# Two attention blocks with Fourier convolutions on one core: transposes in row halves, X in quarters, one batch's x by DRAM, and a new order of the steps

## The chip, the cores and the metric

The kernel runs on one core of a Trainium2 chip. The metric is the device time of one execution in microseconds; the time before is the median of three runs. The profile shows one execution, taken by the hardware profiler, with a span of 457.4 us. TensorE is called PE there, VectorE DVE, ScalarE ACT, GpSimd POOL and SyncE SP; PEld is TensorE's weight load.

## The reference

x has the shape (2, 56, 128, 128), float32: 2 batches of 56 planes of 128 x 128. Two layers of the same form, each with weights of its own, run after one another. In short:

```python
def fno_layer(x, w, b, sw, sb, norm=False, act=False):
    y = spectral_conv(x, w, b)      # rfft2, 2 x 16 x 16 modes mixed, irfft2
    if norm:
        y = inorm(y)
    y = y + skip1x1(x, sw, sb)
    return gelu(y) if act else y

xn = inorm(xa, g1, b1)              # xa: each plane an item of its own
k, q, v = (fno_layer(xn, ...) for K, Q, V)             # 8 heads each
attn = softmax(qh @ kh.T / sqrt(H * W))                # 56 x 56 per head
out = fno_layer(heads of attn @ vh, P...)
att = inorm(out + xa, gan, ban)
h = fno_layer(inorm(att, g2, b2), M0..., norm=True, act=True)
h = fno_layer(h, M1..., norm=True)
y = inorm(h, gmo, bmo) + att
```

What matters for the kernel: the Fourier convolutions touch only 512 modes a plane, the attention is a 56 x 56 matrix per head and batch, and all means and variances can be had from modes and from Gram matrices. So few passes over the planes remain: one that turns x to the front and takes statistics, one that makes the gelu, one that turns its result back and transforms it, and one that makes the layer's output.

## The kernel before

**Layout.** The planes of both batches lie in one buffer, X2: partition 64c + k holds plane k (56 of them) and one of two values c of a row index, so each row of X2 holds two image rows, one in each half of the partitions. The partitions 56 to 63 of each half are padding; row 56 carries a vector of scales. P[b] is a work buffer for each batch, xr holds three slices of 1024 columns for the x that is added at a layer's end, WU and WT hold built weights and later the intermediate results of the transforms. PSUM is handed out as single banks (two) and as pairs of banks (three).

**Steps.** Each piece of work is a Python generator, one for each layer and batch, with a letter. A `yield` ends one step. The string ORDER lists all steps of all generators, by letter and by 2 x layer + batch, so `t2` is a step of "turn" in layer 2, batch 0. At the end `_in_order` ties every engine to the order in which its instructions were written, so ORDER sets the queue of each engine.

- W, R, O, A, B, C: weights. GpSimd prepares the raw weights (prepare), TensorE spreads them over partitions (relay, L376), GpSimd builds the mode matrices (build, L387, and build_m).
- t, k, m, n, g, c: turn (transposes of X2, L412 in layer 1 and L414 in layer 2, ScalarE copies to P[b]), count (statistics, L425), the modes (L518, L435), normalise, the Gram matrix (L569) and its chain.
- q, u, s, v, a, d, p: scale_x (GpSimd scales X2 in place, L609), attention scores and values, softmax, heads and the norms. At the end of `values`, eight transposes of the modes (L694) give XT; at the end of softmax_chain eight products of XT with the matrix BT (L741) give pb.
- y, z, b, f, h: gelu (synthesis L816, mixed L831, gelu L847), its statistics (L854), turn_back (transposes L863, ScalarE copies L864), forward (L881) and the chain to the second norm (transposes of VectorE at L895, sums L487, inverse L452 and L457).
- x, e, o: the end of a layer. end_x fetches x (layer 1, by DMA from the input, L963; layer 2, by a GpSimd multiplication that undoes the scaling of X2, L969); end_sums makes synthesis and products, in layer 2 with a product that adds xr (L989); end_out finishes on VectorE (L1000), and in layer 1 GpSimd adds xr and writes X2 (L1002), while layer 2 sends the result out (L1005).

The transposes of layer 1's turn take 56 rows of either half of the partitions by themselves, each at a tile position of its own. The other transposes of planes (L414, L863) take 120 rows, both halves with the padding between, at once. The initial transfers are queued on SyncE: six of the eight parts of batch 0's x, then all constants but the identity in one transfer (L231, 888.5 KB), then the rest of batch 0, the small parameters and the raw weights of layer 1, and batch 1.

Of the kernel before, what the change touches and what calls it, by code (L numbers as in the profile page):

```python
# [37 lines left out]
F32 = mybir.dt.float32  # L38
# [11 lines left out]
for _name, _n in (  # L50
    ("ident", N), ("fw", 32), ("fh", N), ("gw", N), ("group", N), ("dup", N), ("ext", N), ("fold", 64),
    ("raw", 56), ("count", 8), ("syn", 1), ("same", 32), ("m8", 8), ("sel", 135), ("pick", 32), ("n2", 1), ("fx", N), ("gh", 2 * N),
):
    _PARTS[_name] = (sum(n for _, n in _PARTS.values()), _n)
# [89 lines left out]
t0 t0 t0 t0 t0 W0 t0 k0 k0 k0 k0 k0 t0 t0 k0 k0 k0 m0 m0 m0 W0 m0 m0 n0 n0 n0 t1 t1 t1 t1 m0 k1 k1 k1 t1 t1 m0 m0 W0  # L144
W0 t1 t1 W0 R0 R0 n0 n0 n0 R0 R0 R0 B0 k1 k1 g0 g0 k1 k1 g0 g0 g0 k1 g0 m1 B0 m1 g0 g0 A0 c0 m1 m1 C0 n1 n1 u0 u0 m1
n1 m1 n1 A0 A0 m1 n1 n1 q1 u0 u0 u0 g1 g1 m1 g1 g1 g1 c0 g1 g1 s0 A0 s0 s0 g1 B0 B0 x0 c1 u1 u0 q0 u0 u0 u1 u1 u1 u1
c0 C0 W1 W1 s1 s0 s0 s0 a0 s1 s1 W1 u1 u1 u1 O0 v0 a0 v0 v0 v0 v0 a0 W1 s1 W1 c1 x0 s1 c1 s1 a1 d0 d0 d0 d0 a0 a0 q0
v1 a1 p0 p0 v1 v1 p0 p0 q0 q0 v1 p0 v1 a1 d1 d1 d1 p0 p0 q0 a1 q0 d1 a1 p0 p0 R1 p1 q0 q0 R1 p1 p1 p1 y0 y0 y0 p1 b0
R1 R1 b0 z0 p1 p1 R1 R1 R1 y0 y0 y0 f0 f0 f0 q1 q1 q1 q1 p1 b0 b0 y0 y0 C1 z0 y0 f0 f0 q1 q1 q1 b0 b0 f0 z0 y0 y0 y0
f0 b0 z0 f0 b0 z0 p1 z0 z0 z0 f0 y1 y1 y1 f0 f0 y1 y1 y1 y1 y1 y1 b1 f0 h0 z1 z1 h0 h0 b1 h0 h0 h0 z1 z1 f1 f1 z1 f1  # L150
y1 h0 y1 y1 z1 z1 z1 b1 b1 h0 h0 f1 f1 b1 b1 f1 h0 f1 f1 f1 b1 h0 h0 b1 f1 h0 f1 f1 h1 h1 e0 e0 o0 e0 e0 o0 h1 h1 x0
x0 x0 e0 o0 x0 e0 o0 x0 t2 k2 A1 h1 h1 e0 h1 e0 o0 e0 o0 h1 h1 x0 e0 e0 o0 x1 t2 h1 e0 o0 h1 h1 h1 k2 t2 k2 A1 A1 A1
t2 t2 k2 x1 k2 e1 e1 e1 x1 t2 t2 o1 o1 t2 x1 e1 e1 e1 k2 k2 o1 o1 e1 k2 e1 e1 x1 o1 x1 m2 x1 x1 e1 o1 e1 o1 e1 m2 t3
o1 k3 m2 m2 m2 m2 n2 n2 n2 t3 t3 m2 t3 m2 k3 n2 k3 k3 B1 B1 t3 t3 t3 t3 k3 g2 g2 g2 g2 g2 k3 k3 g2 g2 u2 u2 k3 m3 m3
u2 u2 u2 m3 n3 m3 n3 m3 m3 n3 g2 c2 n2 n2 n3 m3 n3 m3 g3 g3 g3 g3 g3 c2 g3 B1 g3 g3 s2 s2 s2 s3 c3 u2 u2 u2 c2 s2 B1
O1 q2 q2 s2 c3 s2 q2 q2 u3 u3 q2 u3 u3 q2 u3 s3 s3 a2 u3 C1 v2 v2 v2 a2 u3 u3 v2 c3 s3 s3 v2 s3 a3 v3 v3 d2 d2 a2 d2
d2 a2 a2 p2 v3 a3 p2 p2 a3 p2 a3 v3 p2 v3 d3 d3 p2 p2 p2 n3 d3 d3 a3 p3 q2 q2 y2 y2 y2 p3 p3 p3 y2 y2 y2 b2 p2 x2 b2
z2 q3 q3 q3 q3 p3 y2 y2 q3 y2 f2 f2 b2 f2 b2 p3 p3 f2 f2 q3 f2 b2 b2 y2 q3 y2 z2 y2 z2 p3 f2 f2 b2 z2 z2 p3 b2 f2 q3
y3 y3 z3 x2 y3 z3 f2 f2 b3 y3 b3 y3 y3 f3 f3 b3 b3 z2 z2 f3 f2 h2 h2 x3 y3 h2 h2 y3 y3 z2 h2 f3 f3 f3 b3 y3 y3 z3 z3
z3 y3 f3 b3 b3 z3 f3 b3 f3 f3 f3 f3 h3 h3 h3 h2 h2 h2 h3 z3 z3 h3 h3 h3 h2 h3 h3 h2 h3 h2 h2 x2 x2 h3 h2 e2 e2 e2 e2  # L160
e2 x2 x2 x2 e2 o2 o2 o2 o2 h3 h3 e2 x2 e2 e2 x2 e2 e2 x3 e2 e3 e3 x3 x3 o2 x3 e3 x3 e3 e3 x3 o2 o2 o2 o3 o3 o3 e3 e3
e3 x3 e3 e3 o3 e3 x3 o3 o3 o3 e3 o3
# [19 lines left out]
def fno_layers(ctx: ExitStack, tc: tile.TileContext, x, out, weights, small, const):  # L182
# [10 lines left out]
    pq = pool("pair", 3, space=bass.MemoryType.PSUM)  # L193

# [22 lines left out]
    ident = C["ident"]  # L217
    S.dma_start(out=ident, in_=const["all"][:, :N])
# [4 lines left out]
    for b in range(B):  # L223
        for g in range(0, 8, 2):
            for c in range(2):
                Q.dma_start(
                    out=X2[64 * c : 64 * c + K, b, 8 * g : 8 * g + 16, :].rearrange("p (g r) w -> p g (r w)", r=8),
                    in_=xin[c, b, :, g : g + 2, :],
                )
            if (b, g) == (0, 4):  # L230
                Q.dma_start(out=Ct[:, N:], in_=const["all"][:, N:])  # L231
        if b == 0:
            for n in range(2):
                Q.dma_start(out=smt[n], in_=small[n : n + 1, :].to_broadcast([N, N_SMALL]))
            Q.dma_start(out=stage[:, :1088], in_=weights[0].rearrange("p m r n t -> p (m r n t)"))
# [17 lines left out]
    xr = cp.tile([N, 3, 1024], F32, name="xr")  # L253
    G.memset(xr.rearrange("p a b -> p (a b)"), 0.0)
# [145 lines left out]


    def turn(L, b):
        for g in range(8):
            p = pair()
            for s in range(2):
                for e in range(4):
                    i = 8 * g + 4 * s + e
                    if L == 0:
                        for c in range(2):
                            q = slice(64 * c, 64 * c + K)  # L410
                            o = K * (4 * s + e)
                            T.transpose(p[:, c, o : o + K], X2[q, b, i, :], ident[q, q], tile_position=(64 * c, 0))  # L412
                    else:
                        T.transpose(p[:, s, N * e : N * e + 120], X2[:120, b, i, :], ident[:120, :120])  # L414
            dst = P[b][:, 896 * g : 896 * g + 896].rearrange("p (x c k) -> p x c k", x=8, c=2)
            if L == 0:
                S.copy(dst.rearrange("p x c k -> p c x k"), p[:, :, :448].rearrange("p c (x k) -> p c x k", x=8))  # L417
            else:
                S.copy(dst, p.rearrange("p s (e c k) -> p (s e) c k", e=4, c=2)[:, :, :, :K])
            yield  # L420
# [196 lines left out]
    def room(b):  # L617
        R = P[b]
        return {
            "VT": R[:, :4096].rearrange("p (t m) -> p t m", t=4), "XT": R[:, 4096:5120].rearrange("p (t m) -> p t m", t=8),  # L620
            "AT": R[:, 5120:5344], "xs": R[:, 5344:5800], "SC": grid(R[:, 6912:7168], 4), "SG": grid(R[:, 7352:7800]),
            "MI": grid(R[:, 7800:8024], 4), "UX": [R[:, 896 * j : 896 * j + 896] for j in range(2)],
        }
# [52 lines left out]
    def values(L, b):  # L676
# [15 lines left out]
        p = pair()  # L692
        for t in range(8):
            T.transpose(p[:K, t // 4, N * (t % 4) : N * (t % 4) + N], xv[:, t, :], ident)  # L694
        S.copy(R["XT"][:K].rearrange("p t m -> p (t m)"), p[:K].rearrange("p j m -> p (j m)"))
        yield

    def softmax_chain(L, b):
# [40 lines left out]
        pb = s["pair"][:, 1]  # L739
        for t in range(8):  # L740
            T.matmul(pb[:, K * t : K * t + K], lhsT=XT[:K, t, :], rhs=BT[:, :K], start=True, stop=True)  # L741
        yield

    def heads(L, b):
        R = room(b)
        AT, VT = grid(R["AT"], 4), R["VT"].rearrange("p t (e u a m) -> p t e u a m", e=2, u=2, a=4)
        st[L][b]["pair"] = pair()
        p = st[L][b]["pair"][:, 0]
# [13 lines left out]
    def norms_chain(L, b):  # L762
        s, (par, d, _), R = st[L][b], prs[L], P[b]
        D, pb = s["D"], s["pair"][:, 1]
        Pm, u, y0, sqy, s1 = (R[:, 448 * j : 448 * j + 448] for j in range(5))
        bm = R[0:1, 5800:5856]
        V.tensor_tensor(Pm, pb[:, :448], D, ALU.add)
# [3 lines left out]
        V.tensor_tensor(pb[:, :448], pb[:, :448], Pm, ALU.add)  # L771
        V.tensor_tensor(u, pb[:, :448], D, ALU.mult)
# [84 lines left out]
    def turn_back(L, b):  # L857
        for n in range(8):
            p = pair()
            for r in range(2):  # L860
                for e in range(4):
                    o = 512 * r + N * e
                    T.transpose(p[:, r, N * e : N * e + 120], h3(b, n)[:120, o : o + N], ident[:120, :120])  # L863
            S.copy(  # L864
                hT[n % 2].rearrange("p r e c k -> p (r e) c k"),
                p.rearrange("p r (e c k) -> p (r e) c k", e=4, c=2)[:, :, :, :K],
            )
            yield
# [81 lines left out]
    far = [t.rearrange(f, A=4, j=4, c=2) for t, f in zip((x, out), forms)]  # L950

    def end_x(L, b):

        if L == 1:
            p = bank()
            T.matmul(p[:, :N], lhsT=st[L][b]["gv"].to_broadcast([N, N]), rhs=ident, start=True, stop=True)
            inv = st[L][b]["gvr"]
            V.reciprocal(inv, p[:, :N])
            yield
        for n in range(8):  # L960
            if L == 0:
                for c in range(2):
                    Q.dma_start(  # L963
                        out=xr[64 * c : 64 * c + K, n % 3, :].rearrange("p (r m) -> p r m", r=2),
                        in_=far[0][b, c, :, n // 2, 2 * (n % 2) : 2 * (n % 2) + 2],
                    )
            else:
# [4 lines left out]
                )  # L972
            yield

    def end_sums(L, b):
        s = st[L][b]
        for A in range(4):
# [4 lines left out]
            for v in range(2):  # L982
                n = 2 * A + v
                mixed(L, b, A, v, both[v], Be_[b], L == 0)
                if L == 1:
# [10 lines left out]
    def end_out(L, b):  # L996
        s = st[L][b]
        for n in range(8):
            h, p = h3(b, n), s["ends"][n]
            V.scalar_tensor_tensor(h, h, s["hs"], p.rearrange("p r m -> p (r m)"), ALU.mult, ALU.add)  # L1000
            if L == 0:
                G.tensor_tensor(X2[:, b, 8 * n : 8 * n + 8, :].rearrange("p e w -> p (e w)"), h, xr[:, n % 3, :], ALU.add)  # L1002
            else:
                for c in range(2):
                    Q.dma_start(  # L1005
                        out=far[1][b, c, :, n // 2, 2 * (n % 2) : 2 * (n % 2) + 2],
                        in_=h[64 * c : 64 * c + K].rearrange("p (r m) -> p r m", r=2),
# [75 lines left out]
```

## Time and profile before

Time before: 463.39 us, the median of 463.01, 463.39 and 463.41.

| Row of the profile | Count | Busy us | Mean ns |
|---|---|---|---|
| L863, TensorE transposes 120 x 128 of turn_back | 256 | 31.1 | 271 |
| L414, TensorE transposes 120 x 128 of layer 2's turn | 128 | 16.1 | 275 |
| L412, TensorE transposes 56 x 128 of layer 1's turn | 256 | 14.9 | 271 |
| L694, TensorE transposes 128 x 56 for XT | 32 | 4.2 | 276 |
| L741, TensorE products with BT | 64 | 8.0 | 275 |
| L989, TensorE products that add xr | 128 | 16.6 | 589 |
| L969, GpSimd multiplications for xr | 16 | 37.3 | 2360 |
| L1002, GpSimd additions of xr | 16 | 37.4 | 2369 |
| L1000, VectorE, end of a layer | 32 | 40.4 | 1275 |

How to read it: a matrix product in float32 shows as two records, a transpose as one. The busy time of a TensorE row is the union of records that overlap, so it is not the time that the row holds up the engine. Mean is the length of one record. The planes' transposes have nearly the same mean in both forms; how far apart they start is seen in the timeline alone. A line number belongs to the kernel before.

### The profile page before, as it was taken

What the parts mean: (1) busy time and instruction counts of PE and PEld (TensorE: products, weight loads), DVE (VectorE), ACT (ScalarE), POOL (GpSimd) and SP (SyncE); (2) the same over time, 40 slices, a digit from 0 to 9 for tenths busy, and PEclk for the clock granted to TensorE, in tenths of its full rate; (3) what the DMA queues carried; (4) which work ended last, traced back from release to release, by engine and by line L of the source; (5) the groups of instructions that cost most, each with busy time, mean ns of one, the idle gap of its engine ahead of it and who ended that gap; (6) DMA issues with size and microseconds to landing.
All of it is one profiled execution on the core that took longest, in us unless ns stands there. A gap on an engine that the chain in (4) does not pass through costs nothing.

```text
span 457.4 us, 14855 instructions
## 1 busy us (share of the span) xinstructions
PE 404.3 (88%) x6724; PEld 285.7 (62%) x6724; DVE 264.5 (58%) x457; ACT 186.8 (41%) x250; POOL 251.6 (55%) x263
## 2 busy tenths in 40 slices
PE   2347889999999999999899989999999999869994
PEld 1324668779886665756654858878857665554441
DVE  1438933114444479799889942223626788776653
ACT  2336333483404565612322634684265565320000
POOL 2089677999933930029889405954099200006693
PEclk9999899998978999999999999999979999859998
DMA  8999600000010020005444000000000000003565
GB/s 185 233 224 197 128 3 4 3 4 3 3 7 0 2 49 1 2 1 163 120 122 123 4 3 5 3 3 3 7 3 7 1 1 2 2 0 99 172 204 173
DMA packets 9887, 25.97 MB, mean 57 GB/s; under 512 B 1616, under 2 KB 2256, under 8 KB 9808
## 3 DMA queue, kind: packets, MB, share of 16 engines
q1 hardware_dynamic: 9680, 24.96, 22.0%
q8 instruction: 52, 0.85, 0.8%
q10 hardware_dynamic: 144, 0.07, 0.1%
q14 instruction: 11, 0.09, 0.1%
HBM read 17.42 MB, written 7.34 MB: 54 GB/s over the span
## 4 chain that ended last, share of the span: by engine, by line
PE 67%; DVE 14%; DMA 5%; POOL 5%; ACT 5%; issue 3%; SPq 0%; ACTq 0%; DVEq 0%; POOLq 0%
PE pair L831 11%; PE pair L816 8%; PE bank L569 7%; PE pair L863 6%; DMA sm<-small 4%; DVE P L1000 3%; PE pair L752 3%; PE pair L989 3%; PE pair L685 3%; PE pair L636 3%; PE bank L881 3%; PE bank L487 3%; PE bank L663 2%; PE pair L452 2%; PE bank L376 2%
## 5 line engine op out<-in xcount | busy, mean ns | idle before, releaser
L609 POOL TENSOR_TENSOR X<-X,gvr 120x1024 f32<-120x1024 f32 x32 | 74.6, 2351 | 5.1 <-ACT gvr L561 5.1
L1002 POOL TENSOR_TENSOR X<-P,xr 128x1024 f32<-128x1024 f32 x16 | 37.4, 2369 | 42.6 <-DVE P L1000 41.5
L969 POOL TENSOR_TENSOR xr<-X,gvr 120x1024 f32<-120x1024 f32 x16 | 37.3, 2360 | 31.2 <-PE pair L989 31.2
L1000 DVE SCALAR_TENSOR_TENSOR P<-P,hs,pair 128x1024 f32<-128x1024 f32 x32 | 40.4, 1275 | 18.7 <-PE pair L989 16.9
L425 DVE BATCH_NORM_STATS2 stats<-P 128x6 f32<-128x448 f32 x64 | 34.7, 612 | 18.3 <-ACT P L417 18.3
L854 DVE BATCH_NORM_STATS2 stats<-P 128x6 f32<-128x512 f32 x64 | 39.2, 676 | 3.8 <-ACT P L847 3.8
L847 ACT ACTIVATE P<-pair 128x1024 f32<-128x1024 f32 x32 | 31.0, 1022 | 17.0 <-PE pair L831 16.9
L831 PE MATMUL pair<-X,Bs 57*64 57x512 f32 x256 | 35.0, 663 | 0.0
L864 ACT COPY WT<-pair 128x896 f32<-128x896 f32 x32 | 28.1, 907 | 15.0 <-PE pair L863 14.9
L831 PE MATMUL pair<-X,Be 57*64 57x512 f32 x256 | 33.8, 617 | 0.0
L569 PEld LDWEIGHTS bank<-P 128*64 128x64 f32 (+1 forms) x1024 | 31.0, 138 | 3.1 <-issue 1.7
L569 PE MATMUL bank<-P 128*64 128x56 f32 (+1 forms) x1024 | 31.7, 222 | 0.5 <-DVE own L534 0.3
L863 PEld LDWEIGHTS pair<-C,P 120*128 120x128 f32 x256 | 26.3, 141 | 9.1 <-issue 6.2
L412 PE MATMUL pair<-C,X 56*128 56x56 f32 x256 | 14.9, 271 | 19.1 <-DMA X<-x 12.7
L863 PE MATMUL pair<-C,P 120*128 120x120 f32 x256 | 31.1, 271 | 0.8 <-ACT P L847 0.7
L412 PEld LDWEIGHTS pair<-C,X 56*128 56x128 f32 x256 | 12.6, 178 | 23.3 <-DMA X<-x 10.6
L387 POOL TENSOR_TENSOR WT<-tc,C 128x1024 f32<-128x1024 f32 x8 | 15.5, 1952 | 16.0 <-PE bank L435 11.9
L816 PEld LDWEIGHTS pair<-C,WT 32*128 32x128 f32 x512 | 17.2, 188 | 11.2 <-DVE P L1000 6.7
L417 ACT COPY P<-pair 128x896 f32<-128x896 f32 x16 | 13.9, 905 | 21.9 <-PE pair L412 21.9
L816 PE MATMUL pair<-C,WT 32*128 32x128 f32 x512 | 20.9, 288 | 1.7 <-DVE WT L457 1.1
L816 PE MATMUL pair<-C,P 32*128 32x128 f32 x512 | 22.1, 302 | 0.1
L816 PEld LDWEIGHTS pair<-C,P 32*128 32x128 f32 x512 | 18.8, 201 | 3.4 <-issue 2.5
(242 smaller groups left out, 820.2 us busy)
## 6 DMA issues: line engine op xcount, KB each, us to landing
X<-x SPq DMA_DIRECT2D x16, 448.0 KB
xr<-x SPq DMA_DIRECT2D x32, 224.0 KB
out<-P SPq DMA_DIRECT2D x32, 224.0 KB
stage<-weights SPq DMA_DIRECT2D x2, 544.0 KB
C<-const_all SPq DMA_DIRECT2D x1, 888.5 KB
X<-x SPq DMA_DIRECT2D x2, 256.0 KB
X<-gvr SPq DMA_DIRECT2D x8, 32.0 KB
sm<-small SPq DMA_DIRECT2D x2, 63.0 KB
```

The costliest lines, as they stand in the source:

```text
L425: V.bn_stats(stats[:, n, :], P[b][:, 448 * n : 448 * n + 448])
L569: T.matmul(p[u : u + m, :K], lhsT=P[b][:, K * i : K * i + m], rhs=plane[b][:, i, :], start=(i < 2), stop=(i == N - 1), tile_position=(0, u ...
L609: G.tensor_tensor(v, v, _bc(gvr[:120], 1, 8), ALU.mult)
L816: T.matmul(both[j // 2][:, j % 2, N * e : N * e + N], lhsT=Z[32 * j : 32 * j + 32, o : o + N], rhs=C["gw"][32 * j : 32 * j + 32, :], start ...
L831: T.matmul(p[64 * c : 64 * c + 64, r, :], lhsT=Bs[q, :], rhs=X2[q, b, s : s + 4, :].rearrange("p e w -> p (e w)"), start=False, stop=stop, ...
L847: S.activation(h3(b, 2 * A + v), both[v].rearrange("p r m -> p (r m)"), AF.Gelu)
L854: V.bn_stats(stats[:, 2 * n + r, :], h3(b, n)[:, 512 * r : 512 * r + 512])
L863: T.transpose(p[:, r, N * e : N * e + 120], h3(b, n)[:120, o : o + N], ident[:120, :120])
L864: S.copy(hT[n % 2].rearrange("p r e c k -> p (r e) c k"), p.rearrange("p r (e c k) -> p (r e) c k", e=4, c=2)[:, :, :, :K],)
L969: G.tensor_tensor(xr[:120, n % 3, :].rearrange("p (c s w) -> p c s w", c=2, s=4), x8.rearrange("p (c v s) w -> p v c s w", c=2, v=2)[:, n ...
L1000: V.scalar_tensor_tensor(h, h, s["hs"], p.rearrange("p r m -> p (r m)"), ALU.mult, ALU.add)
L1002: G.tensor_tensor(X2[:, b, 8 * n : 8 * n + 8, :].rearrange("p e w -> p (e w)"), h, xr[:, n % 3, :], ALU.add)
```

## The change

It has six parts.

1. **Transposes in row halves.** A helper `turned` does what layer 1's turn did: two transposes of 56 rows, at tile positions (0, 0) and (64, 0), into the two banks of a pair. Layer 2's turn and turn_back now use it too. The ScalarE copies read the banks in that layout. It is meant to let the two halves of the array load and run beside one another.
2. **X in quarters.** XT is made of 64-row transposes at two tile positions, and copied to both halves of the partitions by two ScalarE copies; its products with BT become 16 products of 56 rows and 64 columns at four tile positions, which read BTx (a copy of BT on both halves) and write both banks of a pair of their own.
3. **x of batch 0 in layer 2 by DRAM and GpSimd.** Layer 1's output of batch 0 is also stored in a DRAM buffer. In layer 2 it is read back into xr, and GpSimd adds it to the result, as in layer 1; the multiplication on GpSimd and the products at L989 fall away for this batch. Batch 1 stays as it was.
4. **Constants later.** 160 columns that are needed first come ahead of the last part of batch 0's x; all other constants come after it. "group" is moved next to "fw" for that.
5. **The order is new.** ORDER has the same steps, apart from the counts that part 3 changes, in a new sequence. Among others, batch 0's Gram matrix now precedes the relay of the weights; in layer 2 batch 0's last chain (h2) lies between steps of batch 1's gelu and forward (y3, f3), and its ends (e2, o2) between steps of batch 1's chain (h3).
6. A list of input and output views by batch, and `from_x2`, which tells which way x comes.

```diff
-    ("ident", N), ("fw", 32), ("fh", N), ("gw", N), ("group", N), ("dup", N), ("ext", N), ("fold", 64),
+    ("ident", N), ("fw", 32), ("group", N), ("fh", N), ("gw", N), ("dup", N), ("ext", N), ("fold", 64),
...
 ORDER = """
-t0 t0 t0 t0 t0 W0 t0 k0 k0 k0 k0 k0 t0 t0 k0 k0 k0 m0 m0 m0 W0 m0 m0 n0 n0 n0 t1 t1 t1 t1 m0 k1 k1 k1 t1 t1 m0 m0 W0
-W0 t1 t1 W0 R0 R0 n0 n0 n0 R0 R0 R0 B0 k1 k1 g0 g0 k1 k1 g0 g0 g0 k1 g0 m1 B0 m1 g0 g0 A0 c0 m1 m1 C0 n1 n1 u0 u0 m1
...
-y3 y3 z3 x2 y3 z3 f2 f2 b3 y3 b3 y3 y3 f3 f3 b3 b3 z2 z2 f3 f2 h2 h2 x3 y3 h2 h2 y3 y3 z2 h2 f3 f3 f3 b3 y3 y3 z3 z3
-z3 y3 f3 b3 b3 z3 f3 b3 f3 f3 f3 f3 h3 h3 h3 h2 h2 h2 h3 z3 z3 h3 h3 h3 h2 h3 h3 h2 h3 h2 h2 x2 x2 h3 h2 e2 e2 e2 e2
-e2 x2 x2 x2 e2 o2 o2 o2 o2 h3 h3 e2 x2 e2 e2 x2 e2 e2 x3 e2 e3 e3 x3 x3 o2 x3 e3 x3 e3 e3 x3 o2 o2 o2 o3 o3 o3 e3 e3
-e3 x3 e3 e3 o3 e3 x3 o3 o3 o3 e3 o3
+t0 t0 t0 t0 W0 t0 t0 t0 x0 k0 k0 k0 k0 k0 k0 k0 t0 k0 m0 m0 m0 n0 m0 n0 m0 m0 W0 W0 W0 t1 W0 k1 n0 m0 m0 n0 n0 t1 t1
+t1 g0 g0 g0 g0 k1 k1 k1 g0 R0 g0 n0 q0 q0 t1 t1 t1 t1 R0 R0 k1 k1 k1 R0 k1 m1 R0 A0 A0 A0 g0 g0 c0 c0 m1 u0 u0 m1 n1
...
+f2 q3 b2 y3 b2 y3 x2 z3 y3 z3 f2 f2 f2 b3 y3 b3 y3 y3 h2 h2 h2 h2 f3 f3 f3 y3 y3 y3 z3 h2 z3 z3 h2 b3 b3 h2 z3 f3 f3
+f3 b3 b3 h2 h2 y3 y3 f3 h2 y3 b3 h2 h2 h2 f3 f3 b3 f3 f3 e2 e2 f3 e2 e2 e2 e2 e2 h3 o2 x2 o2 x2 o2 x2 h3 h3 h3 z3 o2
+x2 z3 h3 e2 h3 h3 x3 e2 o2 x2 h3 h3 e2 e2 e2 o2 h3 o2 h3 h3 h3 x3 o2 x3 x3 e3 e3 o3 e3 e3 e3 x3 e3 x3 x3 x3 e3 e3 e3
+e3 e3 o3 o3 x3 o3 o3 o3 o3 e3 o3
 """
...
+    first = 2 * N + 32
...
-                Q.dma_start(out=Ct[:, N:], in_=const["all"][:, N:])
+                Q.dma_start(out=Ct[:, N:first], in_=const["all"][:, N:first])
         if b == 0:
+            Q.dma_start(out=Ct[:, first:], in_=const["all"][:, first:])
...
+    store = dp.tile([1, K, N, N], F32, name="store0")
...
+    def turned(p, o, rows):
+
+        for c in range(2):
+            q = slice(64 * c, 64 * c + K)
+            T.transpose(p[:, c, o : o + K], rows[q, :], ident[q, q], tile_position=(64 * c, 0))
+
...
-                    else:
-                        T.transpose(p[:, s, N * e : N * e + 120], X2[:120, b, i, :], ident[:120, :120])
+                    turned(p, K * (4 * s + e), X2[:, b, i, :])
...
-            T.transpose(p[:K, t // 4, N * (t % 4) : N * (t % 4) + N], xv[:, t, :], ident)
-        S.copy(R["XT"][:K].rearrange("p t m -> p (t m)"), p[:K].rearrange("p j m -> p (j m)"))
+            for e in range(2):
+                q, o = slice(64 * e, 64 * e + 64), 256 * (t % 2) + 64 * (t // 2)
+                T.transpose(p[:K, e, o : o + 64], xv[q, t, :], ident[q, q], tile_position=(64 * e, 0))
+        for c in range(2):
+            S.copy(
+                R["XT"][64 * c : 64 * c + K].rearrange("p e t m -> p e (t m)"), p[:K, :, 256 * c : 256 * c + 256],
+            )
...
-        pb = s["pair"][:, 1]
-        for t in range(8):
-            T.matmul(pb[:, K * t : K * t + K], lhsT=XT[:K, t, :], rhs=BT[:, :K], start=True, stop=True)
+        pb = s["pb"] = pair()
+        for t in range(4):
+            for c in range(2):
+                q = slice(64 * c, 64 * c + K)
+                for e in range(2):
+                    T.matmul(
+                        pb[64 * e : 64 * e + 64, c, K * t : K * t + K], lhsT=XT[q, e, t, :], rhs=BTx[q, :K],
+                        start=True, stop=True, tile_position=(64 * c, 64 * e), skip_group_check=True,
+                    )
...
-                    T.transpose(p[:, r, N * e : N * e + 120], h3(b, n)[:120, o : o + N], ident[:120, :120])
+                    turned(p, K * (4 * r + e), h3(b, n)[:, o : o + N])
             S.copy(
-                hT[n % 2].rearrange("p r e c k -> p (r e) c k"),
-                p.rearrange("p r (e c k) -> p (r e) c k", e=4, c=2)[:, :, :, :K],
+                hT[n % 2].rearrange("p r e c k -> p c (r e) k"),
+                p[:, :, :448].rearrange("p c (x k) -> p c x k", x=8),
             )
...
+    def from_x2(L, b):
+
+        return L == 1 and b == 1
+
     def end_x(L, b):
 
-        if L == 1:
+        if from_x2(L, b):
...
+        src = far[0][b] if L == 0 else between[1]
...
+            else:
+                for c in range(2):
+                    Q.dma_start(
+                        out=xr[64 * c : 64 * c + K, n % 3, :].rearrange("p (r m) -> p r m", r=2),
+                        in_=src[0, c, :, n // 2, 2 * (n % 2) : 2 * (n % 2) + 2],
+                    )
...
-                mixed(L, b, A, v, both[v], Be_[b], L == 0)
-                if L == 1:
+                mixed(L, b, A, v, both[v], Be_[b], not from_x2(L, b))
+                if from_x2(L, b):
...
-            if L == 0:
-                G.tensor_tensor(X2[:, b, 8 * n : 8 * n + 8, :].rearrange("p e w -> p (e w)"), h, xr[:, n % 3, :], ALU.add)
-            else:
+            X, to = (X2[:, b, 8 * n : 8 * n + 8, :].rearrange("p e w -> p (e w)"), between[0]) if L == 0 else (h, far[1][b])
+            if not from_x2(L, b):
+                G.tensor_tensor(X, h, xr[:, n % 3, :], ALU.add)
+            if L == 1 or b == 0:
                 for c in range(2):
                     Q.dma_start(
-                        out=far[1][b, c, :, n // 2, 2 * (n % 2) : 2 * (n % 2) + 2],
-                        in_=h[64 * c : 64 * c + K].rearrange("p (r m) -> p r m", r=2),
+                        out=to[0, c, :, n // 2, 2 * (n % 2) : 2 * (n % 2) + 2],
+                        in_=X[64 * c : 64 * c + K].rearrange("p (r m) -> p r m", r=2),
                     )
```

## The prediction

> **What bounds the kernel now.** I read the page first: shares of each engine, then the span in 40 slices.
>
> ```profile
> PE 404.3 (88%) x6724; PEld 285.7 (62%) x6724; DVE 264.5 (58%) x457; ACT 186.8 (41%) x250; POOL 251.6 (55%) x263
> ...
> PE   2347889999999999999899989999999999869994
> ...
> POOL 2089677999933930029889405954099200006693
> PEclk9999899998978999999999999999979999859998
> DMA  8999600000010020005444000000000000003565
> ...
> PE 67%; DVE 14%; DMA 5%; POOL 5%; ACT 5%; issue 3%; SPq 0%; ACTq 0%; DVEq 0%; POOLq 0%
> ```
>
> TensorE is full from slice 8 on, except around slices 35 and 36, where its granted clock falls too. The last line, the chain that ended last, runs over TensorE for 67% of the span. So I cut the span at the seams of its stages and asked for the busy times of each stretch:
>
> ```profile
> core 0: us, PE busy (x) PEld busy (x) DVE busy (x) ACT busy (x) POOL busy (x), PEclk, DMA share, GB/s
> 0.00:24.00 24.00, 7.34 (x99) 6.19 (x101) 6.83 (x14) 6.56 (x7) 3.21 (x15) 1.00 0.88 211
> 24.00:54.00 30.00, 20.89 (x221) 13.05 (x221) 21.97 (x32) 14.56 (x16) 24.85 (x58) 0.94 0.92 185
> 54.00:200.00 146.00, 139.69 (x2593) 107.22 (x2595) 72.52 (x144) 70.05 (x96) 86.59 (x106) 0.95 0.04 9
> 200.00:258.00 58.00, 53.91 (x647) 33.64 (x640) 53.37 (x77) 19.43 (x26) 48.28 (x23) 0.97 0.38 105
> 258.00:387.00 129.00, 125.21 (x2467) 94.11 (x2465) 67.17 (x131) 69.88 (x91) 58.06 (x48) 0.97 0.03 4
> 387.00:412.00 25.00, 18.12 (x190) 13.26 (x190) 18.71 (x44) 6.22 (x15) 0.31 (x1) 0.73 0.00 1
> 412.00:453.00 41.00, 39.15 (x522) 18.22 (x522) 23.94 (x19) 0.16 (x1) 30.29 (x13) 1.00 0.55 164
> ```
>
> Six stages: loading (transfers at 0.9 share), the middles of layers 1 and 2 (54 to 200, 258 to 387; TensorE 96% busy, nothing else above 60%), the seam of the layers (200 to 258; VectorE 53.4 and GpSimd 48.3 of 58 stand beside TensorE), two statistics chains after one another (387 to 412; TensorE half waiting, clock 0.73), and the tail. TensorE time saved is worth its full price only in the middles.
>
> Busy time of pipelined matmuls overstates, so prices come from runs of one kind in TensorE's timeline (start, length, count; the step is the length less one matmul's own, over the count less one):
>
> ```profile
> 39.70 1.52 PE L412 MATMUL pair<-C,X 56*128 56x56 f32 x32
> ...
> 45.41 1.20 PE L412 MATMUL pair<-C,X 56*128 56x56 f32 x31 [1.66 <-DMA X<-x]
> ...
> 97.88 1.06 PE L694 MATMUL pair<-C,xf 128*56 128x128 f32 x8
> ...
> 107.14 1.99 PE L741 MATMUL pair<-BT,P 56*128 56x56 f32 x16
> ...
> 360.25 1.86 PE L863 MATMUL pair<-C,P 120*128 120x120 f32 x16
> ...
> 390.02 1.14 PE L471 MATMUL pair<-xf,WM 64*64 64x56 f32 x32 [0.63 <-ACT xf L904]
> ...
> 431.16 18.57 POOL L969 TENSOR_TENSOR xr<-X,gvr 120x1024 f32<-120x1024 f32 x8 [2.33 <-PE pair L989]
> ```
>
> A whole-row transpose (L863): (1.86-0.27)/15 = 106 ns. A half-row one (L412, layer 1's form): (1.20-0.27)/30 = 31 ns and (1.52-0.27)/31 = 40 ns.
>
> **What the Trainium skill says.** (1) "TensorE: Matmul & The Clock Gate", section "The mechanism": a weight load overlaps running matmuls only where it goes to another row group. The trace agrees: two halves in different row groups take 62 to 80 ns, one whole transpose 106. (2) "TensorEngine Tiling (Array Packing)", section "Key Properties": changing the tiling mode drains TensorE. The new transposes stand between 32-row and 64-row work either way; no row here isolates such a drain, and I charge nothing. (3) "GPSIMD Engine Reference", section "Elementwise — side-by-side cycle accounting": two-input operations cost about 2.6 cycles an element whatever they compute. The trace agrees: multiply 2360 ns (L969), add 2369 ns (L1002), so swapping one for the other is free in sum. [...]Here 4.4 us pass after the last compute (453 to 457.4), with outputs queued; whatever the middle gains, this end stays.
>
> **The change, part by part.**
>
> *Transposes in halves.* Layer 2's turn (16 groups of 8) and turn_back (32 groups, both layers): a group goes from 8 x 106 = 0.85 us to 16 halves, 0.50 to 0.64; saving 0.21 to 0.35, I take 0.26. Turn_back, in the middles: 32 x 0.26 = 8.3 us. Turn, in the seam: 16 x 0.26 = 4.2, of which I count 1.5, since VectorE has 53.4 of 58 us to do there and none of it goes. ScalarE's copies keep their size (L417 905 ns in the new layout, L864 907 in the old): nothing.
>
> *X in quarters.* The transposes of XT go from 8 of about 0.12 us to 16 of 31 to 40 ns: 0.4 to 0.5 saved, x4 = 1.8. The products by BT go from 16 records in 1.99 us to 32 of 64x64x56; the nearest row, L471, takes 1.14 us for 32, and L636, better packed, 0.54. I take 0.8: 1.2 x 4 = 4.8 us (3.4 to 5.8). ScalarE gets two copies of 512 for one of 1024 (1006 ns): perhaps 0.1 each time, beside TensorE work. They now wait for BTx (a ScalarE copy) instead of BT, with one weight load and product ahead of them anyway: L736 today already waits 0.4 us for it, so nothing. The VectorE sums keep 448 columns, strided: nothing. A pair of banks more is taken at that point and heads' own is freed sooner: even.
>
> So the middles: 8.3 + 1.8 + 4.8 = 14.9 us of TensorE time on the path. Chains of single waits won't shrink; I count four fifths, 12 us.
>
> *Loading.* 160 columns of constants come before the last quarter of batch 0's x, the rest after: some 0.8 MB at 211 GB/s, 4 us earlier for batch 0's normalisation (its last transposes start at 23.9 now). Small and stage keep their place behind the same bytes, so GpSimd's weight work still starts at 24 and ends at 45.5. But batch 0's gram (32 ns a record x 256 = 8 us) starts now at 54.3 behind the relay; in the new order it stands ahead of it and can fill TensorE's idle 40 to 50. What follows it (u_x) still needs relay and GpSimd's build. Gain 0 to 8, I take 4.
>
> *x of layer 2, batch 0.* Added: 16 stores and 16 loads of 224 KB (3.67 MB each way). The stores go beside loads in the seam (share 0.38 at 105 GB/s; x3.67 MB over some 25 us adds 150 GB/s, near the 211 to 233 GB/s of the start, still under), the loads beside outputs in the tail (164 GB/s). SyncE queues each load behind the store that waits for the same GpSimd add, which the load must wait for as well. Nothing. Removed: 8 x 0.86 = 6.9 us of fold products (L989) in the tail. GpSimd: 8 multiplies become 8 adds.
>
> *Tail.* Before, the forward ends at 387.7, then 25 us of both chains, 41 us of ends, 4.4 us of transfer: 69.7 us. In the new order batch 0's chain lies beside batch 1's gelu and forward, and its ends beside batch 1's chain. Then GpSimd has, from the first result, 8 adds and 8 multiplies = 16 x 2.36 = 37.8 us, 3.4 before (synthesis 1.17, mixed 0.95, VectorE 1.28) and about 7 after (fold, VectorE, transfer): 48 us. By TensorE: chain 25, four steps of 4.7 = 18.8, then 6: 50 us. The chain moved forward still costs TensorE about half of 18.1 at clock 0.73: 6.6 us at full clock. Saved: 69.7 - 50 - 6.6 = 13; I take 12, the 6.9 included.
>
> Sum: 12 + 1.5 + 4 + 12 = 29.5 us; 463.4 - 29.5 = **434 us**.
>
> **The rivals.** *Absorbed* (0.20): freed TensorE time turns into waits for GpSimd and for the chains, clock lower for it. For it: GpSimd 86.6 of 146 us in layer 1's middle and waits of up to 39 us elsewhere; against it: 96% on TensorE. Half of each: 6 + 0.5 + 2 + 6 = 14.5, so 449 us. *All of it* (0.12): 14.9 + 4 + 7 + 14 = 40, so 423 us. *Slower* (0.10): GpSimd becomes the bound of the tail. It made 3 of its 16 multiplies ahead of 387; now all its tail work comes after the first e2 result, since the adds need that and hold the three xr buffers. If the chains still end together at 412, its 37.8 us run from 417 to 455, and 7 us more give 462 instead of 457.4; with stores delaying the seam and nothing gained above, 463.4 + 4.6 = 468 us. Against it: TensorE needs no xr for batch 0 any more, so the ends can run ahead.
>
> **How the numbers follow.** The forecast has 0.58. Its sizes alone run from 425 to 444; the absorbed case reaches to 453 and the full one to 419; left out are the slower case and the outer halves of those two's edges, about 0.2 in all. Range 419 to 453. Faster by over 0.2%: 0.58 + 0.20 + 0.12 = 0.90, less a sliver: 0.89; within 0.2%: 0.02; slower: 0.09.
>
> **What would show it.** TensorE busy should fall by 20 to 30 us. Transposes of turn_back: steps of 31 to 40 ns, 512 of them. L741's successor: 32 records in 0.5 to 1.1 us. L989's: 64 records. Batch 0's gram before 50 us. The low-clock stretch of 25 us before the tail gone or short, GpSimd nearly solid through the tail. I am wrong if halves in turn_back step at 50 ns or more (loads of a row group not overlapping in that surrounding), if TensorE's waits for GpSimd or for ScalarE's copies grow by 10 us, or if GpSimd's first add of the tail starts less than 45 us ahead of the end only because everything before it slipped.

## The result and the profile after

The changed kernel takes **439.42 us** (median of 4 runs, 436.31 to 441.94), the kernel before 463.2 (4 runs, 460.5 to 463.41). The ratio is **0.9496**, 95% interval 0.9426 to 0.9567: 23.8 us less, 5.4 above the forecast of 434 and inside its range. A comparison leaves out disturbed runs, so a ratio can rest on fewer runs than the median beside it.

The page of the changed kernel (span 434.4 us), the lines that answer to those of before:

```profile
PE 374.3 (86%) x7138; PEld 262.9 (61%) x7138; DVE 260.5 (60%) x456; ACT 188.0 (43%) x254; POOL 254.3 (59%) x263
...
PE   2457498999999999989689999999989999887894
...
POOL 2059769999898800045919674998950000065893
PEclk9999789999999999999569999999996999999598
DMA  7999820000020010018736220000021000048465
...
PE 58%; DVE 15%; issue 13%; DMA 6%; POOL 4%; ACT 3%; SPq 0%; DVEq 0%; POOLq 0%; ACTq 0%
```

TensorE is busy 30.0 us less; the others are within 4 us of before. New is the hole in the fifth slice of the PE row (the 4 after 2457, 43 to 54 us). The clock's dip ahead of the tail has shrunk to one slice, the 38th, but a new one stands in slices 20 and 21, the seam. The 13% "issue" of the chain is no idle TensorE: most of it is one stretch of 39 us in layer 1 where the chain was followed along GpSimd, for which the profile shows no wait there; TensorE was busy meanwhile.

Busy times by stretch, cut at the same events as before: the gap in the loading, layer 1's middle in two parts (to its first gelu product, to the end of its forward), the seam, layer 2's middle, and the tail in two parts. Columns as before.

```profile
41.00:54.00 13.00, 7.09 (x183) 6.90 (x181) 5.48 (x7) 1.81 (x3) 10.71 (x24) 0.83 0.92 136
84.40:130.70 46.30, 45.15 (x1168) 38.95 (x1168) 19.06 (x49) 24.27 (x38) 43.65 (x61) 1.00 0.07 14
130.70:186.00 55.30, 53.11 (x867) 32.61 (x863) 41.68 (x76) 35.03 (x42) 18.50 (x11) 1.00 0.04 4
186.00:246.90 60.90, 53.26 (x750) 32.67 (x750) 51.60 (x75) 18.16 (x25) 38.68 (x23) 0.86 0.52 160
246.90:378.90 132.00, 125.13 (x2780) 94.05 (x2776) 74.53 (x150) 76.63 (x103) 62.70 (x46) 0.97 0.07 14
378.90:407.40 28.50, 22.72 (x295) 14.11 (x293) 24.69 (x39) 3.78 (x8) 18.04 (x9) 0.89 0.60 184
407.40:434.40 27.00, 21.01 (x256) 9.37 (x256) 11.15 (x9) 0.00 (x0) 19.54 (x9) 0.88 0.54 165
```

So the two profiled runs differ as follows (ends read from the timelines; the forecast column is the prediction's sum, with the 6.6 us of the moved chain booked where they went):

| Stage | Before, us | After, us | Change | Forecast |
|---|---|---|---|---|
| start to the end of layer 1's Gram products | 82.3 | 84.4 | +2.1 | -4 |
| to the end of layer 1's forward | 117.1 | 101.6 | -15.5 | -6 |
| seam, to layer 2's first Gram product | 58.8 | 60.9 | +2.1 | -1.5 |
| to the end of layer 2's forward | 129.5 | 132.0 | +2.5 | -6 + 6.6 |
| to the end of the program | 69.7 | 55.5 | -14.2 | -18.6 |
| sum | 457.4 | 434.4 | -23.0 | -29.5 |

The new operations cost what was forecast or a little less. TensorE's timeline of the changed kernel, layer 2:

```profile
316.72 0.69 PE L750 MATMUL pair<-BTx,P 56*64 56x56 f32 x32
...
365.63 1.20 PE L409 MATMUL pair<-C,P 56*128 56x56 f32 x32
```

A half transpose steps at (1.20-0.27)/31 = 30 ns, just below the 31 to 40 forecast, so a group of sixteen halves takes 0.48 us where eight whole ones took 0.85; and 32 products with BTx take 0.69 us (0.8 taken, 1.99 before).

### The profile page after: what moved, and what is told of

The parts are those of the page before. It is cut to its first block, busy times and chain, and to the rows that moved or that the text cites. A ratio compares the mean times of both kernels' runs of the same rounds, so it can differ in the third digit from the quotient of the medians.

```text
span 434.4 us, 15733 instructions
## 1 busy us (share of the span) xinstructions
PE 374.3 (86%) x7138; PEld 262.9 (61%) x7138; DVE 260.5 (60%) x456; ACT 188.0 (43%) x254; POOL 254.3 (59%) x263
## 4 chain that ended last, share of the span: by engine, by line
PE 58%; DVE 15%; issue 13%; DMA 6%; POOL 4%; ACT 3%; SPq 0%; DVEq 0%; POOLq 0%; ACTq 0%
PE pair L843 8%; PE bank L570 8%; PE pair L828 5%; PE pair L409 5%; DMA X<-x 4%; PE pair L686 4%; POOL X L610 3%; PE pair L637 3%; DVE P L1018 3%; PE bank L664 3%; PE pair L453 3%; DVE WT L526 3%; PE pair L763 2%; PE bank L436 2%; PE pair L519 2%
## 5 line engine op out<-in xcount | busy, mean ns | idle before, releaser
L1021 POOL TENSOR_TENSOR P<-P,xr 128x1024 f32<-128x1024 f32 x8 | 18.8, 2359 | 65.8 <-issue 59.0
L420 ACT COPY P<-pair 128x896 f32<-128x896 f32 x32 | 27.9, 909 | 46.0 <-PE pair L409 46.0
L409 PE MATMUL pair<-C,X 56*128 56x56 f32 x512 | 26.4, 256 | 17.0 <-DMA X<-x 9.3
L570 PE MATMUL bank<-P 128*64 128x56 f32 (+1 forms) x1024 | 33.7, 230 | 6.6 <-issue 5.9
L409 PEld LDWEIGHTS pair<-C,X 56*128 56x128 f32 x512 | 23.1, 166 | 24.6 <-DMA X<-x 8.9
L843 PE MATMUL pair<-X,Bs 57*64 57x512 f32 x256 | 33.0, 606 | 1.0 <-DMA X<-gvr 1.0
L828 PE MATMUL pair<-C,WT 32*128 32x128 f32 x512 | 23.2, 305 | 3.5 <-DVE WT L458 2.0
L409 PEld LDWEIGHTS pair<-C,P 56*128 56x128 f32 x512 | 19.1, 143 | 10.4 <-issue 4.4
L409 PE MATMUL pair<-C,P 56*128 56x56 f32 x512 | 22.1, 232 | 1.2 <-DVE WU L948 0.5
L519 PE MATMUL pair<-P,fwg 128*32 128x448 f32 x128 | 15.2, 595 | 5.3 <-ACT fwg L507 2.1
```

The costliest lines, as they stand in the source:

```text
L409: T.transpose(p[:, c, o : o + K], rows[q, :], ident[q, q], tile_position=(64 * c, 0))
L570: T.matmul(p[u : u + m, :K], lhsT=P[b][:, K * i : K * i + m], rhs=plane[b][:, i, :], start=(i < 2), stop=(i == N - 1), tile_position=(0, u ...
L828: T.matmul(both[j // 2][:, j % 2, N * e : N * e + N], lhsT=Z[32 * j : 32 * j + 32, o : o + N], rhs=C["gw"][32 * j : 32 * j + 32, :], start ...
L843: T.matmul(p[64 * c : 64 * c + 64, r, :], lhsT=Bs[q, :], rhs=X2[q, b, s : s + 4, :].rearrange("p e w -> p (e w)"), start=False, stop=stop, ...
L1021: G.tensor_tensor(X, h, xr[:, n % 3, :], ALU.add)
```

## The experiments

In a table below a **full-clock span** stands beside the time: the span of a run times its mean granted clock, then the median over the runs. It is a rough measure of work without the clock's share: it takes too much out where TensorE only waits at a low clock. own_pair_in_before shows how well it holds: its 12 runs lie between 450.97 and 464.72 us at clocks between 0.936 and 0.97, its full-clock spans between 432 and 438. In the runs of the kernel before (without one far slower run) a clock lower by 0.01 goes with 3.8 us, by a straight line through them, where the measure takes out 4.8. A difference of 2 or 3 us between medians of four runs is therefore not sharp.

**1 to 3. The TensorE parts in the old order.** halves_in_before makes only this edit (and the copies' layout), in turn and in turn_back; quarters_in_before takes part 2 alone; both_in_before takes both.

```diff
-                    T.transpose(p[:, r, N * e : N * e + 120], h3(b, n)[:120, o : o + N], ident[:120, :120])
+                    turned(p, K * (4 * r + e), h3(b, n)[:, o : o + N])
```

> The kernel before with the transposes in halves alone (turn of layer 2 and turn_back), its old order kept. Theory 1 (TensorE time in the middles is worth its price): 32 groups of turn_back at 0.26 us, four fifths counted, and 1.5 us in the seam: 8 us less than before, so a ratio of 0.983. Theory 2 (the gain is the new order's, freed TensorE time alone turns into waits): at most 2 us less, ratio 0.996 or more, with ScalarE's wait for the transposes shrinking and other waits of TensorE growing by the same amount.

> The kernel before with X in quarters alone, old order. Theory 1: 1.8 + 4.8 us of TensorE time, four fifths: 5 us less, ratio 0.989; the products with BT take 32 records in about 0.8 us where 16 took 1.99. Theory 2: these stand in chains of single waits in which TensorE has other work at hand, so 2 us or less, ratio 0.996 or more.

> The kernel before with halves and quarters, old order. Theory 1: the two add up, 13 us, ratio 0.971. Theory 2: 4 us at most, ratio 0.991 or more. In between, the sum of the two single runs would say that they are independent; less than the sum, that another engine takes over.

Measured: 0.9915 (0.9879 to 0.9951), 0.9821 (0.9777 to 0.9865) and 0.9687 (0.961 to 0.9763); against 460.23 us, the kernel before beside them, these are 3.9, 8.2 and 14.4 us. The sum was about right (12 + 1.5 forecast), its division was not: the halves brought half of the 8 us expected of them, X more than its 5.

**4 and 5. The order by itself.** old_order is the changed kernel with the ORDER of before; new_order_in_before is the kernel before with the new ORDER, cut to its own step counts:

```diff
...
-e3 x3 e3 e3 o3 e3 x3 o3 o3 o3 e3 o3
+e3 e3 o3 o3 x3 o3 o3 o3 o3 e3 o3
```

In both, some slices of x that layer 2 adds for batch 0 are fetched out of turn with their use, so these adds take other values; the work is the same.

> The changed kernel with the old order of steps: halves, quarters, x of batch 0 of layer 2 by DRAM and the constants split, but batch 0's last chain beside batch 1's as before. Theory 1: the 13 us of the first two parts, and of the tail only what the dropped products give, at most 6.9 us, less what GpSimd takes since its adds start only with the first result: 447 to 452 us. If the order is what frees the tail, this stays 8 us or more above the changed kernel's 439. Rival: the order is worth little and this comes within 3 us of 439.

> The kernel before with the new order of steps alone (the steps that fetch x for batch 0 of layer 2 put behind its scaling, since they multiply here). Theory 1: the tail shortens since batch 0's chain is hidden, but the 6.9 us of products and the 13 us of the first two parts are still there: 450 to 456 us. Theory 2 (the order is the gain): 445 us or less. If the order fits the new parts alone, 460 us or more.

Measured: 1.0215 (1.0145 to 1.0285) and 1.0035 (1.0002 to 1.0069). The new order alone gains nothing: its tail is 4.9 us shorter (394.8 to 459.6 us), but layer 2's middle, which took in the chain, is 9.1 longer (256.2 to 394.8).

The old order with all new parts is slower than before by 2%, 17 us above the highest time expected. both_in_before tells which part does it: with the old order and parts 1 and 2 it took 445.54 us, so parts 3 and 4 on top cost 23.7 us there (6.9 by the full-clock spans, 420.6 and 427.5; the rest is clock). The seam takes 65.7 instead of 58.9 us, the tail 80.8 instead of 69.7. In the tail of old_order TensorE waits for GpSimd's xr, which both_in_before does not; total, times and longest wait from 385 to 466 us:

```profile
PE pair L1007 <- POOL xr L981: 8.0, 3, 4.5
```

This is what the prediction's "slower" rival described (GpSimd "becomes the bound of the tail", 468 us), though in the old order, of which it did not speak. So part 3 needs the new order: there it does no harm (runs 8 and 9). Fetches out of turn and the later constants are not separated from it here. The new order in turn pays only beside the other parts: fold_right (runs 8 and 9), which has it with parts 1, 2 and 4, comes to 0.9539 against 0.9687 for both_in_before (full-clock spans 415.1 and 420.6). Why it needs them was not found.

**6 and 7. Parts 1 and 2 taken out of the changed kernel**, with the lines of before restored (the first line of the diff above for whole_in_after; the eight whole products for oldx_in_after):

```diff
-                    turned(p, K * (4 * r + e), h3(b, n)[:, o : o + N])
+                    T.transpose(p[:, r, N * e : N * e + 120], h3(b, n)[:120, o : o + N], ident[:120, :120])
```

> The changed kernel with whole-row transposes again in layer 2's turn and in turn_back, new order kept. Theory 1: 8 us slower than the changed kernel, 447 us; up to 12.5 if the seam and all of the middles pay. Theory 2: within 2 us of 439.

> The changed kernel with XT and its products as before the change, new order kept. Theory 1: 5 us slower than the changed kernel, 444 us. Theory 2: within 2 us of 439.

Measured: 0.9708 (0.964 to 0.9775) and 0.9668 (0.9578 to 0.9758), so beside 0.9496 the halves are worth 2.1%, 9.8 us, in the new order, and X 1.7%, 8 us. Why did the halves bring only 3.9 us in the old order? Layer 1 from its first gelu product to the end of its forward, in windows of four kernels; first the kernel before, then with halves:

```profile
138.50:199.40 60.90, 59.70 (x740) 38.32 (x736) 41.98 (x75) 34.74 (x43) 18.98 (x10) 0.98 0.05 10
```
```profile
137.40:198.70 61.30, 58.31 (x868) 36.61 (x864) 42.05 (x76) 34.87 (x43) 19.01 (x10) 0.92 0.05 10
```

then the changed kernel with whole transposes (its halves are the third line of the windows above):

```profile
130.00:189.30 59.30, 58.71 (x741) 36.54 (x735) 42.38 (x76) 35.35 (x42) 18.56 (x11) 1.00 0.03 3
```

In the new order the halves shorten this stretch from 59.3 to 55.3 us, both at clock 1.00: 4.0 for 16 groups, against 16 x 0.26 = 4.2 forecast. (At a lower clock the same steps take longer: fold_right, with halves and the new order, needs 59.3 us here at 0.89.) In the old order it stays at 61 us: 1.4 us less busy TensorE at a clock of 0.92 instead of 0.98, which alone is 61 x 0.06 = 3.7 us, and one new wait for GpSimd's scaling and the scale row brought by DMA:

```profile
165.70 2.38 PE L829 MATMUL pair<-X,Bs 57*64 57x512 f32 x16 [1.36 <-DMA X<-gvr]
```

Single profiles differ by chance in the clock, so here are all runs (each column is a median; the clock is the median of the runs' mean clocks):

| Kernel | Runs | Median us | Clock | Full-clock span | Lost to the clock |
|---|---|---|---|---|---|
| before | 65 | 461.48 | 0.951 | 435.6 | 22.7 |
| halves_in_before | 20 | 457.51 | 0.933 | 424.9 | 30.5 |
| quarters_in_before | 4 | 450.62 | 0.955 | 428.6 | 20.2 |
| both_in_before | 4 | 445.54 | 0.948 | 420.6 | 23.1 |
| new_order_in_before | 20 | 462.69 | 0.954 | 440.7 | 21.2 |
| whole_in_after | 4 | 449.24 | 0.955 | 426.9 | 20.4 |
| after | 4 | 439.42 | 0.942 | 412.5 | 25.6 |
| oldx_in_after | 4 | 446.34 | 0.937 | 416.4 | 28.2 |

At full clock the halves alone are worth 10.7 us in the old order (8.3 + 1.5 at full price); up to 7.8 of them go back because TensorE is granted less clock. In all three pairs that differ by the halves alone the median clock falls with them: 0.951 to 0.933, 0.955 to 0.948, 0.955 to 0.942. Only the first pair has runs enough; in the other two the clocks of single runs overlap (0.940 to 0.964 against 0.937 to 0.950 in the last). Why it falls is not shown. One rival that no run here separates: the saved work leaves TensorE waiting more, and the waits lower the clock. X saves TensorE 4 x (1.06 - 0.63 + 1.99 - 0.69) = 6.9 us. At full clock it is worth 7.0 us alone, 4.3 beside the halves in the old order and 3.9 in the new one, around the 5.3 forecast; in the old order alone 1.2 us come from the clock on top, in the new order about half of its 8 us.

**8 and 9. Part 3 taken out.** from_x2 holds for both batches, so x of batch 0 comes from X2 again; fold_in_after placed those steps too early, so that some adds of batch 0 in layer 2 took slices of x out of turn, and fold_right puts each fetch behind the use of its buffer:

```diff
-        return L == 1 and b == 1
+        return L == 1
```

> The changed kernel with batch 0's x of layer 2 made from X2 again (GpSimd multiplication and products that add xr), its steps put behind the scaling, new order otherwise kept. If the products dropped are what the tail gains: 64 records, 6.9 us of TensorE time; since GpSimd bounds the end, part of it is hidden: 2 to 6 us slower than 439, so 441 to 445. Rival: the ends of batch 0 stall for xr, which GpSimd frees late, and it is 8 us or more slower. If stores and loads of 3.67 MB cost anything in the seam, the seam of this one is shorter than the changed kernel's 60 us.

> The changed kernel with batch 0's x of layer 2 made from X2 again, as in the run before it with this edit, but with each fetch of a slice put ahead of the product that uses it, so that the whole computation is the reference's. Theory 1 (64 products and their places on TensorE's queue): 2 to 7 us slower than the changed kernel, ratio to before 0.954 to 0.965. Rival (slices wait for GpSimd): 8 us or more slower, ratio above 0.967.

Measured: 0.9629 (0.954 to 0.9718) and 0.9539 (0.9459 to 0.9618). Part 3 is worth 0.4%, 2 us, less than its interval can tell from nothing. GpSimd's timeline shows why so little. First the tail of fold_right, then that of the changed kernel:

```profile
381.94 11.76 POOL L981 TENSOR_TENSOR xr<-X,gvr 120x1024 f32<-120x1024 f32 x5 [22.79 <-PE pair L1007]
...
415.77 11.76 POOL L981 TENSOR_TENSOR xr<-X,gvr 120x1024 f32<-120x1024 f32 x5 [6.91 <-PE pair L1007]
```
```profile
391.22 2.36 POOL L1021 TENSOR_TENSOR P<-P,xr 128x1024 f32<-128x1024 f32 x1 [1.60 <-DVE P L1018]
...
408.38 2.35 POOL L1021 TENSOR_TENSOR P<-P,xr 128x1024 f32<-128x1024 f32 x1
410.81 16.25 POOL L981 TENSOR_TENSOR xr<-X,gvr 120x1024 f32<-120x1024 f32 x7
```

In fold_right GpSimd has holes of 22.8, 8.0 (at 401.9, left out above) and 6.9 us: it waits for TensorE's L1007 to free xr, and TensorE sets the end. The dropped products of batch 0 had stood in batch 1's chain: from the end of the forward to batch 1's first synthesis fold_right needs 31.8 us (378.8 to 410.6), the changed kernel 28.5, and the rest is equal (26.8 and 27.0). In the changed kernel GpSimd is solid from 406 to 427, as the slower rival had it, but TensorE ends later still (428.4).

**10. A pair of banks of its own.** One piece of part 2 alone: pb gets its own pair instead of the second bank of heads'. It was to explain why X brought more than forecast.

```diff
-        pb = s["pair"][:, 1]
+        pb = s["pb"] = pair()
```

> The kernel before, in which pb alone gets a pair of banks of its own and heads' pair is freed at the copy of D; transposes, products and order as before. Quarters alone gained 1.8% where their TensorE time came to 5 to 6.6 us (1.1 to 1.4%). Theory 1 (banks are even, the products and transposes are the gain): ratio 0.998 to 1.002. Theory 2 (a pair held through the softmax chain kept other work from starting): ratio 0.990 to 0.995, and the first gelu of layer 1 starts 2 us or more before 138.5.

Measured: 459.86 us, median of 12, against 462.95; the ratio of 0.9825 (0.9768 to 0.9882) rests on 4 of the 12 runs, those with clocks of 0.96 to 0.97. The full-clock span is 434.6 against 435.6: no gain that can be told from none. Layer 1's first gelu did start at 135.3 us, 3.2 before 138.5, as Theory 2 asks; but from the Gram products to it the kernel before ran at clock 0.90 and this one at 0.99, and 56.2 x 0.10 - 51.2 x 0.01 = 5.1 us of clock explain that. Nothing here speaks against the prediction's "even".

**11. The hole in the loading.** From 44.65 us TensorE stands still for 5.9 us in the middle of batch 0's Gram products, waiting for nothing that the profile shows. TensorE's timeline of the changed kernel:

```profile
41.17 3.47 PE L570 MATMUL bank<-P 128*64 128x56 f32 x111
50.55 4.62 PE L570 MATMUL bank<-P 128*64 128x56 f32 x81 [5.91 <-issue]
```

Theory 1: TensorE has run out of instructions, because their fetch queues behind the bulk loads. light_load leaves out half of batch 1's input transfers and puts a constant there:

```diff
+    V.memset(X2[:, 1].rearrange("p a b -> p (a b)"), 0.5)
...
-        for g in range(0, 8, 2):
+        for g in range(0, 8 - 4 * b, 2):
```

> The changed kernel without the loads of batch 1's second half and of its padding rows (VectorE fills batch 1 with a constant ahead of the loads, so batch 1's result is not the reference's). The Gram matrix of batch 0 stood still for 5.9 us at 44.7, with no wait for another engine, while the loads of batch 1 took 0.92 of the transfers' time. Theory 1 (TensorE ran out of instructions, whose transfer queued behind the loads): with the loads over by about 40 us the gap falls below 1 us and the first 256 records of this matrix take about 8 us. Theory 2 (the gap belongs to the engine: a wait that the profile does not show, for GpSimd or a bank): it stays, 4 us or more. In both the total falls by a few us, since batch 1 arrives sooner; the gap tells them apart.

Measured: 0.9389 (0.9325 to 0.9454), and the hole is gone:

```profile
40.87 5.81 PE L570 MATMUL bank<-P 128*64 128x56 f32 x192
```

The trace holds the fetches as transfers on a queue of their own, 16 KB each. In the changed kernel the last one before TensorE goes on started at 46.95 us, when TensorE already stood, and took 1.92 us; 705 of TensorE's records had begun by then. In light_load the like one started at 40.65, after 479 records. Nor does the hole belong to the Gram products: oldx_in_after, with the same loads, runs these 192 records through, and has its hole later, among batch 1's transposes, with a fetch that started at 54.52:

```profile
57.19 1.32 PE L409 MATMUL pair<-C,X 56*128 56x56 f32 x21 [6.03 <-issue]
```

In light_load the Gram products of layer 1 end at 76.8 instead of 84.4 us. (Not all of these 7.6 us are the hole: the 81 records behind it take 4.62 us at a lowered clock, and the later loads are shorter too.)

**12. The wait for batch 1's scale.** In layer 2 the first gelu products of batch 0 wait 0.48 and 0.50 us and start in pieces, since the order gives GpSimd two steps of batch 1's scaling first. q_sorted puts batch 0's eight first:

```diff
-m3 c2 B1 C1 u2 u2 m3 n3 m3 m3 m3 m3 n3 n3 c2 u2 n3 n3 n3 q3 q3 u2 u2 m3 g3 g3 g3 g3 A1 g3 s2 g3 g3 g3 s3 s2 s2 c3 u2
+m3 c2 B1 C1 u2 u2 m3 n3 m3 m3 m3 m3 n3 n3 c2 u2 n3 n3 n3 q2 q2 u2 u2 m3 g3 g3 g3 g3 A1 g3 s2 g3 g3 g3 s3 s2 s2 c3 u2
...
```

> The changed kernel with one edit in the order: the sixteen steps of scale_x in layer 2 keep their places, but all eight of batch 0 come before those of batch 1. In the changed kernel two of batch 1's stood first, and TensorE waited for the scale row of batch 0 (X<-gvr, 4.7 us of the chain at 315.8) before its first gelu of layer 2. Theory 1 (that wait is GpSimd's, and TensorE has nothing else to do then): 2 to 5 us faster than the changed kernel, ratio to before 0.939 to 0.946. Theory 2 (norms of batch 1 follow at the same time anyway, or batch 1's gelu then waits instead): within 1 us of it.

The wait is gone:

```profile
328.10 1.95 PE L843 MATMUL pair<-X,Bs 57*64 57x512 f32 x16
```

and yet 0.9549 (0.948 to 0.9618): no gain. The full-clock span, 411.9 beside 412.5, says the same. The 4.7 us of the expectation were the scale row's transfer in the chain that ended last; TensorE itself had stood for only 1 us of them. A chain that passes through GpSimd there does not mean that GpSimd sets the end.

## Why the prediction was right, and where it was off

**Transposes in halves: right.** 30 ns a half; at full clock 10.7 us in the old order, 8.0 there beside X (428.6 to 420.6), 14.4 in the new one (426.9 to 412.5), against 8.3 + 1.5 at full price. What the sum lacked is the clock: by the same measure 2.9 to 7.8 us were given back. The absorbed rival named that ("clock lower for it"), and in the old order it is what happened.

**X in quarters: right.** 0.63 us for the transposes, 0.69 for the products, 3.9 to 7.0 us at full clock.

**Middles: more than the 12 forecast in the profiled runs.** 15.5 us in layer 1, of which the kernel before had lost 6.8 to the clock (56.2 x 0.10 + 60.9 x 0.02) and the changed one nothing (this differs from profile to profile); layer 2 got 2.5 longer with a chain of an estimated 6.6 moved in, so it gives 4.1.

**The seam: wrong by 3.6 us.** "Turn, in the seam ... I count 1.5": it got 2.1 us longer. The term had VectorE as its limit, and VectorE's 51.6 us did stay, but it left out the clock. This stage ran at 0.97 before, at 0.91 with the halves alone (58.7 us, no gain) and at 0.86 in the changed kernel: 58.8 x 0.03 = 1.8 us lost to the clock before, 60.9 x 0.14 = 8.5 after. In TensorE's timeline of the changed kernel 16 records of one form take 3.69 us at the low clock and 1.95 behind it:

```profile
223.27 3.69 PE L843 MATMUL pair<-X,Be 57*64 57x512 f32 x16
...
228.10 1.95 PE L843 MATMUL pair<-X,Be 57*64 57x512 f32 x16
```

The order and the stores of part 3 are rivals. Five profiles with the old order took 58.7 to 59.4 us here, seven of eight with the new one 60.3 to 61.1. (old_order, with 65.7, is left out.) But fold_in_after and fold_right, which have no stores and the same steps in this stage, differ by 3 us, with a lower clock in the longer one:

```profile
188.90:250.00 61.10, 53.46 (x754) 32.75 (x750) 51.74 (x75) 18.16 (x25) 38.69 (x23) 0.86 0.53 160
188.00:246.10 58.10, 50.96 (x752) 31.72 (x752) 51.18 (x74) 18.16 (x25) 38.76 (x23) 0.91 0.55 168
```

So the clock alone can make the 2.1 us; whether the new order lowers it stays open. The prediction's sum for the transfers was off too, without harm: 105 and 150 GB/s make 255, not "still under" 233, but the page of the changed kernel has 275 and 257 GB/s in two slices of the seam.

**Loading: the step that failed.** "it stands ahead of it and can fill TensorE's idle 40 to 50": the Gram products did start at 41.2 instead of 54.3 us, but TensorE stood for 5.9 us, and layer 1's Gram products ended 2.1 us later than before, where 4 us earlier were forecast. light_load points to the cause: without the loads that compete with the fetch of instructions the hole is gone. How much the later constants give by themselves was not run.

**Tail: 14.2 us instead of 18.6.** By the prediction's own terms: "chain 25, four steps of 4.7 = 18.8, then 6". TensorE's timeline of the changed kernel, the last waits of batch 1's chain, its first synthesis, and the last products:

```profile
402.07 3.36 PE L453 MATMUL pair<-WU,C 64*128 64x224 f32 x16 [2.31 <-DVE WU L950]
...
407.38 2.09 PE L828 MATMUL pair<-C,WT 32*128 32x128 f32 x32 [1.74 <-DVE WT L458]
...
427.38 1.04 PE L1007 MATMUL pair<-xr,C 56*64 56x512 f32 x8
```

Chain 378.9 to 407.4 = 28.5; steps 407.4 to 428.4 = 21.0, the first of them at a low clock (its synthesis takes 2.09 us, the others' 1.17); end 6.0. The chain got longer with batch 0's ends beside it, which VectorE does too: it is busy 24.7 of these 28.5 us, against 18.7 of 25 before, and both waits above are for it. That the hidden work runs on the chain's own engine was not costed. (No run with the new order takes batch 0's ends out of the chain, so this cause is read from the timeline and not tested.) "6.9 included" for the products of L989 was too much: part 3 measured 2 us.

**The sum.** Against 29.5 us the two profiled runs show 23.0: loading 6.1, seam 3.6, tail 4.4 and layer 2's middle 1.9 short, layer 1's middle 9.5 over, most of that the clock's. The signs of two small terms were wrong, and the luck of one large term covered them. The slower rival's GpSimd did become solid at the end, but the bound only in old_order; no run came to the 423 us of the full case.

## What to carry to other kernels

Look at TensorE savings twice, once at full clock and once with the clock that is granted: span times mean clock, over several runs, roughly tells work saved from clock lost. Try each part in both orders: part 3 cost time in the old order and none in the new one. Before counting on early work beside bulk loads, ask whether the engine's instructions can arrive. And when a chain is hidden beside another stage, add up the engine that both use (here VectorE), not only the one that is freed.

## What the runs showed of the hardware

- **Instructions are transfers too.** The page of the changed kernel lists them (packets, MB, share):

```profile
q8 instruction: 56, 0.92, 0.9%
```

  0.92 MB over the 2 x 7138 records of TensorE is 64 bytes an instruction, and 56 blocks are one for every 256. The Trainium skill, "Runtime: NRT & Kernel Launch", section "Instruction fetch mechanics", has the same block size and calls the cost of a boundary "mostly hidden". In the middles the longest such hole is 1.0 us; in the loading, at a DMA share of 0.92, TensorE stood 5.9 us at one boundary.
- **The granted clock has two values in these traces' clock records, full and half.** Half clock comes in stretches of 3.4 us or two, three or four times that; in the changed kernel at 49.7, 206.7, 220.3, 326.1 and 401.2 us. Ahead of four of these five TensorE was busy for at most 0.67 of the last 3.4 us (none of it at 49.7, behind the hole). Waits are not the whole cause: in fold_right the clock is halved from 175.8 to 186.0 us after 6.8 us in which TensorE was busy throughout.
- **Kernels with halves had the lower clock.** Median over their runs: 0.949 to 0.955 for the five kernels with whole transposes, 0.914 to 0.948 for the nine with halves. Yet with halves the stretch from 130.7 to 186 ran at 1.00, so the form alone doesn't lower it. What does was not found.
